# Linear attention and an expert FFN on one core: output weights' operands kept in DRAM, some products' results in one-bank tiles

## The chip, the cores and the metric

The kernel runs on one core of one Trainium2 chip. The metric is the device time of one execution in microseconds; of the kernel before, three runs are given by their median. Within the core, PE is TensorE (matmuls; PEld is its loading of weights), DVE is VectorE, ACT is ScalarE, POOL is GpSimd and SP is SyncE, which here only issues DMAs.

## The reference

4096 tokens of 1024 features are normalised (`xn`). A linear attention and a mixture-of-experts FFN are computed from `xn`, and the output is `x + attention * silu(ffn)`:

```
q, k, v  = xn @ Wq.T + bq, xn @ Wk.T + bk, xn @ Wv.T + bv
phi(t)   = elu(t) + 1
context  = phi(q) * cumsum(phi(k) * v, over tokens) / 8
s        = context @ Wo.T + bo
g        = silu(p * (gelu(xn @ w1.T + b1) @ w2.T + b2))   # tokens that a top-2 router with a capacity keeps
out      = x + s * g
```

All experts share one FFN. A token that no expert keeps has g = 0, so its output is x. The kernel computes attention output and FFN only for a list of 2048 chosen tokens, which the router fills in order of tokens.

## The kernel before, in words

**First part (to 445 us).** For the head of the tokens it normalises, transposes, routes, and computes keys and values with their running sums (`kvs` in DRAM). This part is not changed.

**Second part: 140 products.** The 2048 chosen tokens are handled in two passes of 1024 (`NP` = 2, loop at L1371). A pass is a row of ten big matrix products of 1024 x 1024 x 1024: for each of four quarters of the FFN, `hidden` (1024 hidden units by 1024 tokens) and `ffn_out`; then `queries` and `result`. Each is computed by a scheme with seven half-size products in place of eight (512 x 512 x 512), whose operands are sums of quarters of the two matrices. So a pass has 70 products and the kernel 140. In pass 0, the quarter s has `hidden` at products 14s+1 to 14s+7 and `ffn_out` at 14s+8 to 14s+14; `queries` are products 57 to 63 and `result` 64 to 70.

**One product.** `multiply(n)` (L1010) issues 48 matmuls of 128 x 128 by 128 x 512. An fp32 operand is kept as two fp32r parts: a rounded one, which ACT casts (`Unit.cast`, L799), and the rest, which DVE subtracts (`Unit.low`, L802). Three matmuls (high by high, high by low, low by high) make one fp32 product. An operand comes in two halves u of 8 KB a partition, in three rotating slots per side, so the first half of product n+1 can be made when n begins, and the second when n is done with its first half. Left operands (`a`) are weights in `hidden` and `queries`, tokens' features in `ffn_out` and `result`. Right operands (`b`) are tokens in the former, weights in the latter. The right tokens' seven sums are split once and kept in DRAM (`xtd`); `fetched` (L986) loads them by SP's queue. Those of pass 1 are made in pass 0 by `xprep_items` (L656): four items, each gathering rows, transposing, summing, splitting, and storing seven operands' pieces through POOL's queue. They use the pool `s4` of eight 4 KB buffers (`small`).

**Results.** Several products add into one PSUM tile, a chain. `chains` (L1039) groups them; two tiles of four banks (`fps`) take turns. After product n, DVE or ACT reads its tile in the phase `evac` of n+1.

**The order of the work is written by hand.** For each n, the loop at L1390 issues the matmuls of product n and then runs the hooks of ten phases in order: load, pre, cast0, evac, low0, add, cast1, low1, post, raw. Within a phase they run in the order in which `on` registered them. PE, DVE, ACT and SP keep this order; so does POOL for what is marked `in_turn`. `cast0`, `low0`, `cast1`, `low1` at n make the operands of n+1. The hooks of `xprep_items` are registered at the top of a pass, ahead of all others of that pass.

**Around queries and result.** `queries` calls `features` with `act` (Relu and Exp on ACT, L1248) and `then` (L1260: the rest of elu + 1, then times the running sums, six DVE instructions). `result` (L1300) calls `outputs`, which calls `left_tokens` (L1098: sums of the context's quarters), `right_weights` (L1072: four loads of `wo`, four sums on DVE, and casts and lows of both halves of seven operands; here with `ahead` = 1, so that its first two sums stand in the phase post of product 61) and `chains`. `done` (L1322) adds a finished quarter to `out` by four indirect DMAs of POOL; `last` (L1355) finishes a quarter.

Of the kernel before, what the change touches and what calls it, by code (L numbers as in the profile page):

```python
# [18 lines left out]
P = 128  # L19
# [8 lines left out]
BT = 512  # L28
# [18 lines left out]
def tile_first_tokens(  # L47
# [42 lines left out]


    xtd = [dp.tile([7 * P, 2 * 4 * BT], F32, name=f"xtd_{p}") for p in range(NP)]


    ident = kp.tile([P, P], F32, name="ident")
# [560 lines left out]
    def xprep_items(p, buf):  # L656
# [50 lines left out]

        return [item(j) for j in range(NJ)]


    def kv_srcs(blocks):
        return [w[e] for _ in range(blocks) for e in range(DC) for w in (wk, wv)]
# [66 lines left out]
    def name(n):  # L779
        uid[0] += 1  # L780
        return f"{n}_{uid[0]}"
# [127 lines left out]
        (f"{side}2", fp.tile([P, 2, 2 * BT], F32R, tag=f"{side}2", name=f"{side}2"))  # L909
        for side in "ab"  # L910
    )
    fps = ctx.enter_context(tc.tile_pool(name="fps", bufs=2, space=PSUM, reuse_waits="tile"))
    bq1, nbq = (cp.tile([P, DC], F32, name=n) for n in ("bq1", "nbq"))
    nc.gpsimd.tensor_scalar(bq1, bq, 1.0, None, ALU.add)
    nc.gpsimd.tensor_scalar(nbq, bq, -1.0, None, ALU.mult)
# [4 lines left out]
    def on(n, phase, f):  # L920
        hooks.setdefault((n, phase), []).append(f)
# [61 lines left out]
            on(n - 1, f"cast{u}", cast)  # L983
            on(n - 1, f"low{u}", lambda u=u: units[u].low())

    def fetched(n, p, i):  # L986

        units = plan_at(n)["b"]

        def load():  # L990
            src = tokens(p, i)
            for u in range(2):
                x = units[u] = Unit("b", 2 * n + u)
                nc.sync.dma_start(flat(x), src[u])

        on(n - 1, "load", load)
        plan_at(n)["bview"] = all_chunks

    def tokens(p, i):
        return xtd[p].rearrange("(i p) (u f) -> i u p f", i=7, u=2)[i - 1]  # L1000

    def flat(x):
        return x.t.bitcast(F32).rearrange("p h f -> p (h f)")
# [1 line left out]
    def plan_at(n):  # L1005
        while len(plan) < n:
            plan.append({"a": {}, "b": {}})
        return plan[n - 1]

    def multiply(n):  # L1010
        s = plan_at(n)
        if s["first"]:
            s["ps"][0] = fps.tile([P, 4, BT], F32, tag="ps", bufs=2, name=name("ps"))
        ps = s["ps"][0]
        order_of = [(u, m) for u in range(2) for m in range(4)]
        if n == len(plan):

            order_of.sort(key=lambda um: um[1])
        for u, m in order_of:
            a, b = s["aview"](s["a"][u].t), s["bview"](s["b"][u].t)  # L1020
            for k in range(2):
                for i, (h, l) in enumerate(((0, 0), (0, 1), (1, 0))):
                    nc.tensor.matmul(  # L1023
                        ps[:, m],
                        a(h, k, m),
                        b(l, k),
                        start=s["first"] and u == 0 and k == 0 and i == 0,
                        stop=u == 1 and k == 1 and i == 2,
                        skip_group_check=True,
                    )  # L1030
# [5 lines left out]
    FIRST = (1, 2, 6, 7, 5, 4, 3)  # L1036
    COLS = (1, 2, 6, 5, 7, 3, 4)

    def chains(n0, order, groups):  # L1039
        where = {i: [None] for g in groups for i in g[:1]}  # L1040
        for g in groups:
            for i in g:
                k = order.index(i)
                plan_at(n0 + 1 + k).update(first=i == g[0], ps=where[g[0]])

    def left_weights(n0, src, order):

# [21 lines left out]
        for k, i in enumerate(order):  # L1069
            built(n0 + 1 + k, "a", lambda i=i: q[of[i]], by_blocks, of_blocks)  # L1070

    def right_weights(n0, src, ahead=0):  # L1072

        q = dict(zip(((0, 0), (0, 1), (1, 1), "t", (1, 0)), raw))
        raw[:] = (q[k] for k in ("t", (0, 1), (0, 0), (1, 1), (1, 0)))

        def load(*keys):
            for i, j in keys:
                nc.sync.dma_start(
                    q[i, j].rearrange("p (a k) f -> p a (k f)", a=2),  # L1080
                    src[j, 2 * i : 2 * i + 2].rearrange("a p k f -> p a (k f)"),
                )

        on(n0 - 4, "raw", lambda: load((0, 0), (0, 1)))
        on(n0 - 3, "raw", lambda: load((1, 1)))
        on(n0 - 1, "raw", lambda: load((1, 0)))

        def t1():
            sub(q["t"], q[0, 1], q[0, 0])
            sub(q[0, 1], q[1, 1], q[0, 1])  # L1090

        on(n0 - 1 - ahead, "post" if ahead else "add", t1)
        on(n0, "post", lambda: sub(q[0, 0], q[1, 1], q["t"]))
        on(n0 + 5, "add", lambda: sub(q[1, 0], q[1, 0], q[0, 0]))
        for k, key in enumerate(((0, 0), (1, 0), (0, 0), "t", (0, 1), (1, 1), (1, 0))):
            built(n0 + 1 + k, "b", lambda key=key: q[key], by_chunks, all_chunks)

    def left_tokens(n0, h):  # L1098


        on(n0 + 1, "post", lambda: plus(h["t"], h[0, 1], h[1, 1]))
        on(n0 + 2, "pre", lambda: sub(h[0, 1], h[0, 0], h[0, 1]))
        on(n0 + 2, "pre", lambda: sub(h[0, 0], h["t"], h[0, 0]))
        on(n0 + 4, "add", lambda: sub(h[1, 0], h[1, 0], h[0, 0]))
        for k, key in enumerate(((0, 0), (1, 0), (0, 0), "t", (0, 1), (1, 0), (1, 1))):
            built(n0 + 1 + k, "a", lambda key=key: h[key], by_chunks, of_chunks)

    def right_tokens(n0, p, order):
        if n0:
            for k, i in enumerate(order):  # L1110
                fetched(n0 + 1 + k, p, i)
            return

        x = {(i, j): work[:, 2 * j + i] for i in range(2) for j in range(2)}
        t2 = hq["t"]
        on(3, "add", lambda: sub(x[0, 0], x[1, 1], t2))
        on(4, "add", lambda: sub(x[1, 0], x[1, 0], t2))
        keys = {1: (0, 0), 2: (1, 0), 3: (1, 1), 4: (1, 0), 5: (0, 0), 7: (0, 1)}
        for k, i in enumerate(order):
            built(1 + k, "b", lambda i=i: t2 if i == 6 else x[keys[i]], by_chunks, all_chunks)  # L1120

            def keep(k=k, i=i):
                for u in range(2):
                    nc.sync.dma_start(tokens(p, i)[u], flat(plan_at(1 + k)["b"][u]))

            on(k + 1, "raw", keep)

    def features(n0, p, src, act, then=None, order=ROWS):
# [2 lines left out]
        left_weights(n0, src, order)  # L1131
        right_tokens(n0, p, order)
        if order == ROWS:
            chains(n0, order, ((1, 2), (6, 7, 4), (5, 3)))
        else:
            chains(n0, order, ((1,), (2,), (6, 5, 3), (7, 4)))
        ps = {k: plan_at(n0 + k)["ps"] for k in range(1, 8)}
# [2 lines left out]
            nc.scalar.copy(whole(h[key]), whole(ps[1][0]))  # L1140

        def more(k, key, base):
            plus(h[key], ps[k][0], h[base])

        def c11():
            act(h[0, 0], ps[3][0], 0, 0)
# [22 lines left out]
            on(n0 + 5, "evac", lambda: more(4, (1, 1), (0, 1)))  # L1169
        on(n0 + 6, "evac", lambda: last(5, (1, 1), (1, 1)))  # L1170
        on(n0 + 7, "evac", lambda: last(6, (1, 0), (1, 0)))
        on(n0 + 8, "evac", lambda: last(7, (0, 1), (0, 1)))
        return h

    def over_blocks(row):
# [9 lines left out]
            n0, p, w1[s * DC : (s + 1) * DC], act, order=ROWS if s else FIRST  # L1185
        )

    def outputs(n0, h, src, ahead=0):
        left_tokens(n0, h)
        right_weights(n0, src, ahead)  # L1190
        chains(n0, COLS, ((1,), (2,), (6, 7, 4), (5, 3)))
        return {k: plan_at(n0 + k)["ps"] for k in range(1, 8)}

    def ffn_out(n0, h, s, y):


        ps = outputs(n0, h, w2[s])
        new = list(yq) if s == 0 else []

        def first(k, key, j):  # L1200
# [25 lines left out]
    def queries(n0, p):  # L1226
# [18 lines left out]
                    )  # L1245


        def act(dst, src, i, j):  # L1248
            if dst is src:
                r = [small("ex") for _ in range(2)]  # L1250
                r = [r[m // 2][:, m % 2 * BT : (m % 2 + 1) * BT] for m in range(4)]
            else:
                r = [dst[:, m] for m in range(4)]
            kvt["r", i, j] = r
            for m in range(4):
                e = 4 * i + m
                nc.scalar.activation(r[m], src[:, m], AF.Relu, bias=nbq[:, e : e + 1], scale=-1.0)
                nc.scalar.activation(r[m], r[m], AF.Exp, scale=-1.0)
# [40 lines left out]

    def result(n0, h, y, p):  # L1300

        ps = outputs(n0, h, wo[0], 1)
        c = {}

        def row():
# [13 lines left out]
            c[0] = y[0]  # L1319
            plus(c[0], ps[1][0], over_blocks(c["b"][:, :BT]))  # L1320

        def done(key, parts):  # L1322
            i, j = key
            for m in range(4):
                src = parts(m)
                apart(
                    in_turn(
# [20 lines left out]

        def more(k, key):
            c[key] = h["t" if key == (0, 1) else (0, 1)]  # L1350
            for half in range(2):
                v = slice(2 * half, 2 * half + 2)
                plus(c[key][:, v], ps[k][0][:, v], c[1][half])

        def last(k, key, base):  # L1355
            rows_of = range(4) if n0 + k == len(plan) else [slice(0, 4)]
            for v in rows_of:
                plus(c[base][:, v], ps[k][0][:, v], c[base][:, v])
                nc.vector.tensor_tensor(c[base][:, v], c[base][:, v], y[key][:, v], ALU.mult)
            done(key, lambda m: c[base][:, m])  # L1360

        on(n0 + 2, "evac", e1)
        on(n0 + 3, "evac", c11)
# [6 lines left out]
    n0 = 0  # L1370
    for p in range(NP):  # L1371
        y = dict(yq)
        if p + 1 < NP:
            prep = xprep_items(p + 1, small)
            ats = ((0, 2, 2, 2, 2, 3, 3, 3, 4), (2, 4, 4, 5, 4, 5, 5, 6, 6))
            for j, (s, at) in enumerate((s, at) for s in (1, 2) for at in ats):
                for k, (d, f) in enumerate(zip(at, prep[j])):
                    on(n0 + 14 * s + d, "post" if k else "load", f)
        for s in range(NQ):
            h = hidden(n0, p, s)  # L1380
            ffn_out(n0 + 7, h, s, y)
            n0 += 14
        h = queries(n0, p)
        finals(n0, y, p)
        result(n0 + 7, h, y, p)
        n0 += 14
# [87 lines left out]
```

## Time and profile before

| | |
|---|---|
| median of three runs | 2052.49 us (2051.97 to 2054.68) |
| profiled execution | 2053.1 us, its span 2051.3 us |
| PE busy | 1968.8 us, 96% of the span |
| DVE busy | 1513.0 us, 74% |
| ACT busy | 756.7 us, 37% |
| POOL busy | 398.3 us, 19% |
| matmuls of the products (L1023) | 6720, first at 444.7 us, last at 2029.6 us |
| granted clock, mean | 0.982 |
| DMA | 360.31 MB, 176 GB/s mean |

The span runs from the first to the last instruction of the execution. Busy time is that of an engine's instructions; a busy PE says that matmuls follow each other. A wait is put down to the instruction whose signal came last before the waiting one began. The granted clock is the share of full speed that TensorE was given.

### The profile page before, as it was taken

How to read it: one execution, taken by the hardware profiler on the slowest of the kernel's cores; microseconds unless marked ns; L12 is line 12 of the kernel's file. 1: busy time of each engine (PE TensorE's matmuls, PEld its weight loads, DVE VectorE, ACT ScalarE, POOL GpSimd, SP SyncE). 2: the span in 40 equal slices, each digit the busy share in tenths (PEclk: the TensorE clock that was granted, in tenths of full speed). 3: DMA queues.
4: the chain of work that ended last, by engine and by line, in shares of the span. 5: the costliest groups of instructions: out<-in, count | busy, mean ns of one | idle time of the engine just before them, and what ended most of it. 6: DMA issues, size and time to landing. Idle time of an engine off the chain costs nothing.

```text
span 2051.3 us, 22262 instructions
## 1 busy us (share of the span) xinstructions
PE 1968.8 (96%) x8840; PEld 1624.9 (79%) x8840; DVE 1513.0 (74%) x1378; ACT 756.7 (37%) x874; POOL 398.3 (19%) x359
## 2 busy tenths in 40 slices
PE   7999999999999999999999799999999999999875
PEld 6877878888887887888888578888888888888664
DVE  7868876679867867875877786775774775786784
ACT  2323332225433524433433453342432432433451
POOL 1001104654002402713040027300000003040013
PEclk9999999999999999999999989999999999999988
DMA  8867848657249349347156049427326327336314
GB/s 308 241 195 239 268 124 189 194 153 299 80 166 362 108 164 343 121 153 282 46 184 254 23 110 307 168 75 249 127 87 249 116 100 257 116 124 235 124 21 63
DMA packets 113842, 360.31 MB, mean 176 GB/s; under 512 B 12768, under 2 KB 37344, under 8 KB 95584
## 3 DMA queue, kind: packets, MB, share of 16 engines
q1 hardware_dynamic: 77504, 299.98, 42.2%
q0 software_dynamic: 17792, 42.55, 7.8%
q10 hardware_dynamic: 18432, 16.26, 3.5%
q8 instruction: 72, 1.18, 0.2%
q14 instruction: 42, 0.34, 0.1%
HBM read 292.66 MB, written 73.42 MB: 178 GB/s over the span
## 4 chain that ended last, share of the span: by engine, by line
PE 78%; DVE 11%; ACT 3%; DMA 3%; issue 3%; POOL 0%; ACTq 0%; SPq 0%; DVEq 0%; POOLq 0%
PE ps L1023 62%; PE pk L160 3%; PE pk L161 3%; PE pk L162 3%; PE pv L162 2%; PE pv L160 2%; PE pv L161 2%; DMA b<-xtd 1%; DVE hid L951 1%; DVE a L802 1%; DVE hid L1263 1%; DVE b L802 1%; DVE raw L948 1%; DMA xtd<-b 1%; PE pl L326 1%
## 5 line engine op out<-in xcount | busy, mean ns | idle before, releaser
L1023 PE MATMUL ps<-b,a 128*128 128x512 f32 x6720 | 1541.1, 392 | 44.2 <-DVE y L951 20.7
L1023 PEld LDWEIGHTS ps<-b,a 128*128 128x128 f32 x6720 | 1269.0, 189 | 315.9 <-ACT b L799 21.5
L799 ACT CAST a<-raw 128x1024 fp32r<-128x1024 f32 x140 | 147.2, 1052 | 434.6 <-PE ps L1023 376.1
L802 DVE TENSOR_TENSOR a<-raw,a 128x1024 fp32r<-128x1024 f32 x140 | 170.6, 1221 | 171.2 <-ACT a L799 171.2
L648 POOL DMA_INDIRECT gk<-kvs,eighth x128 | 156.4, 1222 | 657.8 <-DVE kv L240 620.0
L799 ACT CAST a<-hid 128x1024 fp32r<-128x1024 f32 x120 | 126.0, 1050 | 358.0 <-PE ps L1023 250.4
L802 DVE TENSOR_TENSOR a<-hid,a 128x1024 fp32r<-128x1024 f32 x120 | 146.5, 1221 | 63.8 <-ACT a L799 63.6
L802 DVE TENSOR_TENSOR b<-raw,b 128x1024 fp32r<-128x1024 f32 x140 | 170.7, 1220 | 1.9 <-ACT b L799 1.9
L951 DVE TENSOR_TENSOR hid<-ps,hid 128x2048 f32<-128x2048 f32 x54 | 123.5, 2286 | 54.4 <-PE ps L1023 54.4
L948 DVE TENSOR_TENSOR raw<-raw,raw 128x2048 f32<-128x2048 f32 x70 | 160.3, 2289 | 1.0
L799 ACT CAST b<-raw 128x1024 fp32r<-128x1024 f32 x140 | 146.6, 1047 | 2.1 <-DMA xtd<-b 2.1
L951 DVE TENSOR_TENSOR work<-ps,work 128x2048 f32<-128x2048 f32 x40 | 91.5, 2288 | 48.8 <-PE ps L1023 48.8
L160 PE MATMUL pk<-xt,ws_w 128*128 128x512 f32 (+1 forms) x264 | 102.4, 388 | 1.5 <-ACT xt L166 1.5
L161 PE MATMUL pk<-xt,ws_w 128*128 128x512 f32 (+1 forms) x264 | 102.0, 386 | 1.3 <-DVE xt L167 1.3
L162 PE MATMUL pv<-xt,ws_w 128*128 128x512 f32 (+1 forms) x264 | 101.4, 384 | 1.3 <-DVE ws_w L167 1.2
L162 PE MATMUL pk<-xt,ws_w 128*128 128x512 f32 (+1 forms) x264 | 101.8, 386 | 0.0
L160 PE MATMUL pv<-xt,ws_w 128*128 128x512 f32 (+1 forms) x264 | 101.6, 385 | 0.0
L161 PE MATMUL pv<-xt,ws_w 128*128 128x512 f32 (+1 forms) x264 | 101.2, 383 | 0.0
L166 ACT CAST ws_w<-wr_w 128x1024 fp32r<-128x1024 f32 x64 | 66.1, 1049 | 70.0 <-issue 30.8
L167 DVE TENSOR_TENSOR ws_w<-wr_w,ws_w 128x1024 fp32r<-128x1024 f32 x64 | 77.8, 1215 | 14.7 <-ACT ws_w L166 14.7
L680 POOL DMA_DIRECT2D xtd<-o x28 | 24.2, 888 | 283.3 <-DVE o L167 276.3
L362 ACT ACTIVATE kb<-pk,bs 128x512 f32<-128x512 f32 (+1 forms) x40 | 25.8, 645 | 140.8 <-PE pk L162 106.5
(185 smaller groups left out, 1656.4 us busy)
## 6 DMA issues: line engine op xcount, KB each, us to landing
b<-xtd SPq DMA_DIRECT2D x126, 1024.0 KB, 5.5
raw<-in_w SPq DMA_DIRECT2D x64, 1024.0 KB, 5.2
wr_w<-in_wk SPq DMA_DIRECT2D x32, 512.0 KB, 4.6
wr_w<-in_wv SPq DMA_DIRECT2D x32, 512.0 KB, 4.6
xtd<-b SPq DMA_DIRECT2D x14, 1024.0 KB, 7.7
xtd<-o POOLq DMA_DIRECT2D x28, 512.0 KB, 9.1
kvs<-kr ACTq DMA_DIRECT2D x32, 256.0 KB, 4.9
raw<-in_wq SPq DMA_DIRECT2D x8, 1024.0 KB, 5.1
```

Source lines behind the costliest of these rows:

```text
L160: nc.tensor.matmul(ps, ws[:, 0, k], mv[:, 0, k, c0:c1], start=k == 0, stop=False)
L161: nc.tensor.matmul(ps, ws[:, 0, k], mv[:, 1, k, c0:c1], start=False, stop=False)
L162: nc.tensor.matmul(ps, ws[:, 1, k], mv[:, 0, k, c0:c1], start=False, stop=k == DC - 1)
L166: nc.scalar.copy(dst[0], src)
L167: nc.vector.tensor_tensor(dst[1], src, dst[0].bitcast(F32), ALU.subtract)
L362: nc.scalar.activation(kb, ps, AF.Identity, bias=bcol)
L648: nc.gpsimd.indirect_dma_start(out=dst, out_offset=None, in_=src, in_offset=bass.IndirectOffsetOnAxis(ap=idx, axis=0),)
L799: nc.scalar.copy(self.parts[0], src)
L802: nc.vector.tensor_tensor(self.parts[1], self.src, self.parts[0].bitcast(F32), ALU.subtract)
L948: nc.vector.tensor_tensor(dst, a, b, ALU.subtract)
L951: nc.vector.tensor_tensor(dst, a, b, ALU.add)
L1023: nc.tensor.matmul(ps[:, m], a(h, k, m), b(l, k), start=s["first"] and u == 0 and k == 0 and i == 0, stop=u == 1 and k == 1 and i == 2, sk ...
```

## The change

It has these parts.

- **Weights' right operands in DRAM.** `wod`, in DRAM, holds the seven right operands of `wo` in split form. `wprep_items` makes them during pass 0, in four items. An item fetches 4 x 256 KB, forms sums of 128 x 512 (four subtractions), splits seven pieces, and stores each (512 KB) through POOL. The stages stand at products k (fetch, phase load) and k+1, k+1, k+2, k+3, k+4 (phase post) for k = 8, 20, 25, 37, and are registered at the top of pass 0. `result` then takes `right_stored`, which fetches the operands from `wod` with `fetched`, in both passes, in place of `right_weights`.
- **Stages for pass 1's tokens** begin at products 13 and 30 where they began at 14 and 28.
- **Places in PSUM.** A chain's tile is taken from one of two places (`banks`), the one that the preceding product does not write. Where `apart` is set, the tile is four tiles of one bank each: for the chain of products 61 and 63 in `queries` (5 and 3 in the scheme's numbers), and in the last result for the chain of its products 3, 5 and 7. The last product of such a chain computes one block after the other.
- **Reading by blocks.** In `queries`, the last product's quarter is read block by block, each followed by its Relu and Exp: blocks 0 to 2 within product 63 (phases add, low1, post), block 3 in phase pre of 64. In the last result, quarters 5, 6 and 7 of the order are finished and scattered block by block.
- **One subtraction moved.** In `left_tokens`, the sum for `h[0, 1]` is formed one product later, from other terms.

```diff
+    def wprep_items(w, buf):
+        def item(a, k):
+            v = {}
+            def fetch():
+                for j in range(2):
+                    r = buf(f"wr_{a}_{k}_{j}")
+                    for i in range(2):
+                        v[i, j] = r[:, i * BT : (i + 1) * BT]
+                        row = w[j, 2 * i + a].rearrange("p k f -> p (k f)")
+                        in_turn(nc.gpsimd.dma_start(v[i, j], row[:, k * BT : (k + 1) * BT]))
+            def out_of(i, src):
+                o = buf(f"wo_{a}_{k}_{i}")
+                oh = o.bitcast(F32R).rearrange("p (h t) -> h p t", h=2)
+                split((oh[0], oh[1]), src)
...
+                in_turn(
+                    nc.gpsimd.dma_start(dst[:, a, :, k], o.rearrange("p (h t) -> p h t", h=2))
+                )
+            def sums():
+                t = buf(f"wt_{a}_{k}")
+                v["t1"], v["t2"] = t[:, :BT], t[:, BT:]
+                nc.vector.tensor_tensor(v["t1"], v[0, 1], v[0, 0], ALU.subtract)
+                nc.vector.tensor_tensor(v["t2"], v[1, 1], v["t1"], ALU.subtract)
+            def out1():
+                out_of(1, v[0, 0])
+                out_of(2, v[1, 0])
+            def out2():
+                out_of(6, v["t2"])
+                nc.vector.tensor_tensor(v[1, 0], v[1, 0], v["t2"], ALU.subtract)
+                out_of(4, v[1, 0])
+            def out3():
+                out_of(3, v[1, 1])
+                nc.vector.tensor_tensor(v[0, 1], v[1, 1], v[0, 1], ALU.subtract)
+                out_of(7, v[0, 1])
+            def out4():
+                out_of(5, v["t1"])
+            return fetch, sums, out1, out2, out3, out4
+        return [item(a, k) for a in range(2) for k in range(2)]
...
+    def banks(apart):
+        i = last_place[0] = 1 - last_place[0]
+        place = places[i]
+        if place[0] != apart:
+            place[2].close()
+            place[:2] = apart, place[2].enter_context(
+                tc.tile_pool(
+                    name=name("fps"), bufs=1, space=PSUM, side=("left", "right")[i],
+                    reuse_waits="tile",
+                )
+            )
...
     def multiply(n):
         s = plan_at(n)
         if s["first"]:
-            s["ps"][0] = fps.tile([P, 4, BT], F32, tag="ps", bufs=2, name=name("ps"))
+            s["place"][0], s["ps"][0] = banks(s["apart"])
+        last_place[0] = s["place"][0]
...
-        if n == len(plan):
+        if s["apart"] and s["last"]:
...
+    def right_stored(n0, ops):
+        for k, i in enumerate(COLS):
+            fetched(n0 + 1 + k, ops, i)
...
-        on(n0 + 2, "pre", lambda: sub(h[0, 1], h[0, 0], h[0, 1]))
         on(n0 + 2, "pre", lambda: sub(h[0, 0], h["t"], h[0, 0]))
+        on(n0 + 3, "pre", lambda: sub(h[0, 1], h[1, 1], h[0, 0]))
...
-        on(n0 + 8, "evac", lambda: last(7, (0, 1), (0, 1)))
+        if not then:
+            on(n0 + 8, "evac", lambda: last(7, (0, 1), (0, 1)))
+            return h
+        def block(m):
+            key = (0, 1)
+            plus(h[key][:, m], ps[7][0][m], h[key][:, m])
+            act(h[key], h[key], *key, blocks=(m,))
+        for d, phase, m in ((7, "add", 0), (7, "low1", 1), (7, "post", 2), (8, "pre", 3)):
+            on(n0 + d, phase, lambda m=m: block(m))
...
-        ps = outputs(n0, h, wo[0], 1)
+        ps = outputs(n0, h, right_stored, wod, final=p == NP - 1)
...
-            done(key, lambda m: c[base][:, m])
+                done(key, lambda m: c[base][:, m], range(4) if len(parts) == 1 else (v,))
...
+        if p == 0:
+            for k, f in zip((8, 20, 25, 37), wprep_items(wo[0], small)):
+                for d, stage in zip((0, 1, 1, 2, 3, 4), f):
+                    on(n0 + k + d, "post" if d else "load", stage)
...
-            for j, (s, at) in enumerate((s, at) for s in (1, 2) for at in ats):
+            for j, (k, at) in enumerate((k, at) for k in (13, 30) for at in ats):
```

## The prediction

> **What bounds the kernel now.** I read the waits of TensorE first, because PE is busy for 96% of the span and ends the chain of waits. Columns: total us, times, longest.
>
> ```profile
> PE ps L1023 <- DVE y L951: 20.7, 2, 10.5
> PE ps L1023 <- DVE b L802: 8.4, 8, 1.4
> PE ps L1023 <- DVE hid L951: 8.1, 2, 4.0
> PE ps L1023 <- DMA b<-xtd: 5.6, 3, 2.5
> ```
>
> All that the 140 products wait for is here, 44 us, in few places. I then cut the span at the starts of products (every 48th matmul) and read windows. Columns: stretch, length, busy PE, PEld, DVE, ACT, POOL, granted clock, DMA share, GB/s.
>
> ```profile
> 630.20:643.40 13.20, 11.12 (x50) 8.90 (x49) 8.04 (x9) 6.19 (x10) 3.40 (x4) 1.00 1.01 394
> 643.40:656.00 12.60, 12.60 (x49) 10.23 (x50) 8.65 (x10) 4.71 (x7) 2.53 (x3) 0.86 1.02 408
> ...
> 1140.40:1157.50 17.10, 11.60 (x49) 8.67 (x47) 13.11 (x13) 8.07 (x12) 0.00 (x0) 0.96 0.01 1
> 1157.50:1182.60 25.10, 13.18 (x49) 10.13 (x49) 21.02 (x17) 11.40 (x15) 0.00 (x0) 0.77 0.00 0
> 1182.60:1198.10 15.50, 14.09 (x49) 11.02 (x50) 13.65 (x12) 12.82 (x19) 7.22 (x4) 0.76 0.37 50
> 1198.10:1209.00 10.90, 10.90 (x50) 9.03 (x49) 9.19 (x7) 5.55 (x7) 0.00 (x0) 1.00 0.49 126
> ```
>
> An undisturbed product takes 10.88 us (last row). I number products 1 to 140; per pass of 70, queries are 57-63 and result 64-70. Products 64, 65, 66 take 17.2, 25.1 and 15.5; with 1.1 before 62 that is 26.3 us over the 10.88s, and the same stretch of pass 1 loses 26.5. VectorE is full there. Products 18 and 32 wait for DMA and the next ones lose 1.7 each to a half-speed clock: 4.0 and 4.4 us. Product 10 waits 0.7. The timeline shows who is late at the transition:
>
> ```profile
> 1137.07 2.28 DVE L951 TENSOR_TENSOR hid<-ps,hid 128x2048 f32<-128x2048 f32 x1
> ...
> 1155.10 2.28 DVE L951 TENSOR_TENSOR hid<-ps,hid 128x2048 f32<-128x2048 f32 x1
> ...
> 1157.53 0.76 PE L1023 MATMUL ps<-b,a 128*128 128x512 f32 x1 [4.03 <-DVE hid L951]
> ```
>
> Product 63 ended at 1140.7; its result is read only at 1155.10, as VectorE does the query features, a subtraction of output weights and their splits first. Product 65 needs that place. The tail:
>
> ```profile
> 2029.98 0.69 DVE L951 TENSOR_TENSOR y<-ps,y 128x512 f32<-128x512 f32 x1 [6.26 <-PE ps L1023]
> ...
> 2038.19 1.56 POOL L1328 DMA_INDIRECT out<-y,half  x1 [0.30 <-issue]
> ```
>
> The first quarter of the last product is read only when all of it is done (PE ends at 2029.8), though its blocks were computed one after another.
>
> **Part 1: output weights from DRAM.** Per result stage it removes 4 subtractions (2.29) and 14 splits on DVE (1.22), 26.2 us, 14 casts on ACT (1.05), and four 1 MB loads. Once, in pass 0, it adds 28 casts (0.62), 28 lows and 16 subtractions (0.69): ACT 17, DVE 30 us, 16 loads and 28 stores on POOL's queue. DVE falls by 22 us, but only its place counts.
>
> The stored operands come by SP's queue, 2 MB per product. Nearest row: the 1 MB b<-xtd, 5.5 us to landing against 10.9 per product, so hidden; with the next quarter's 1 MB that is 289 GB/s, where 394 was moved above. If that cover were gone, the saturated row below (11.9 us) says some 2.5 per product. Product 62's 1.1 us goes: the wo load at L1079 no longer stands in SP's queue ahead of its b.
>
> **Part 2: the transition, with one-bank tiles and the moved subtraction.** Durations from the timeline: read 2.29, four Relu/Exp pairs 5.1, `then` 5.05, low 1.13, cast 1.05, block read 0.69, block pair 1.3. DVE is free at 1117.8, not 1122.4 (the two weight subtractions, 4.62, are gone).
> - 61 read until 1120.1, ACT pairs 1125.3, cast and low 1127.5, `then` 1132.6.
> - 62 read until 1134.9, left split 1136.0: 64 starts as 63 ends, 1139.2. Blocks 0 and 1 are read by 1137.3, inside product 63. ACT, in order: pairs 1140.1, block 0 1141.5, cast 1142.5, block 1 1143.8. Low 1143.7, `then` 1148.8, blocks 2 and 3 by 1150.2.
> - ACT: last pairs 1152.3, cast of 65's left operand 1153.3, low 1154.5: 65 starts at 1154.5, 4.4 us after 64 ends. Behind the wait for its pairs, DVE has nothing else to do in time.
> - `then` 1160.6, sum 1162.9, one subtraction (two before) 1165.2, both reads of 64 (4.6) 1169.8, low 1171.0: 66 starts at 1171.0 (before: 1182.6 and, after a split, 1184.8).
>
> Clock: the Trainium skill ("TensorE: Matmul & The Clock Gate", Part 1) says that half speed comes after at least one idle window of about 3.4 us. The 643.40 row speaks otherwise: after 2.2 us idle the clock was 0.86 over the product, 1.7 us lost. By the rule 65 (4.4 idle) pays some 2.4 and 66 (3.2 idle) nothing; by the row 66 pays 1.7 too. I take the row: 67 starts at 1171.0 + 10.9 + 1.7 = 1183.6, against 1198.1. Gain 14.5; pass 1, which lost 0.3 more, 14.8. Sum -29.3 (-20 if ACT's order costs a few us more, -36 if no half-speed stretch is left).
>
> A right slot of 64 comes free late, as block order keeps both halves of 63's operands until 7/8 of it: its b lands at 1144.2 for 1144.6. A miss of up to 4 us costs nothing, since 65 waits for DVE anyway.
>
> **Part 3: the tail.** Product 139's blocks are read and scattered one by one from 9.3 us before PE's end T. Eight scatters at 1.87: first issue T-8.6, last T+4.5, still POOL-bound; before, the last issue was T+8.4. -3.9 (0 to -6).
>
> **Part 4: pass 0 pays.** The new stages are registered ahead of the products' own, so they precede them within a phase.
> - Output stages: from product 10 on, DVE has 9.0 of 10.9 us, plus 2.7 per new stage with its wait for ACT. Worked like the above, product 11 is 0.4 late, 24 and 25 0.9 and 0.8: +2.1; product 10's 0.7 goes with the moved subtraction. Bounds -0.7 to +8.
> - The second pair of token items moves from products 28-34 to 30-36. Its DMA no longer meets the 2 MB weight load in 31:
>
> ```profile
> DMA packets 1681, 7.81 MB, mean 391 GB/s; under 512 B 149, under 2 KB 149, under 8 KB 1306
> ...
> b<-xtd SPq DMA_DIRECT2D x4, 1024.0 KB, 11.9
> ```
>
>  That is the DMA view of 625-645: saturated. Products 31 to 34 now ask 4.0, 4.5, 3.5, 4.5 MB = 16.5 MB in 43.5 us (before, 10 MB fell in two products). The skill ("DMA: Bandwidth & Descriptors", Specifications) puts HBM at about 358 GB/s per core: 46.1 us, 2.6 late, which speaks against the move; the row's 394 gives 41.9. I take the row: product 33's 4.4 us goes. The first pair moves by one product only: 17 and 18 still ask 5.5 and 4.5 MB, so 19 stays late, 4.0.
> - But its last stages now fall in products 34-36, where DVE already has 9 us each. In 34: 9.0 + 6.0 (two transposes 1.25, three lows and two sums 0.69) and 1 of waiting for ACT; in 35: 9.0 + 2.8 + 1.9. With 1.4 brought along from 33, the read of product 35 starts 9.0 us into 36 (before, 0.8: 835.17). From there to the split for product 38 it was 19.8 us; minus 2.3 (moved subtraction), plus 2.6 (token stage of 36 ahead of the sum): 20.1. Ready at 29.1, due at 21.8: 7.3 late over products 37 and 38, and some 1.9 of half clock. +9.2 (0 if DMA makes the token stages slip into free time, 14 if 36's lag spreads).
>
> **Edits at nothing.** The choice of place: the waits show none for a place at an output-to-hidden border, so there was no such stall to remove; the same tile was waited for at 65, and is after. The moved subtraction costs nothing in its new phase in passes without new stages: products 24 and 38 have 2.8 and 3.1 us of DVE idle before.
>
> **Sum.** -29.3 - 3.9 + 2.1 - 0.7 - 4.4 + 9.2 = -27.0. The profiled execution took 2053.1 (span 2051.3), 0.6 over the median of 2052.5; off the median: 2025.5.
>
> **Rivals.**
> - *Pass 0 doesn't pay* (0.22): DVE slips the token stages into its 5 us of idle time in 30 and 32. Then +9.2 and +2.1 fall away: 2014. For: 32 and 33 had 5.5 and 3.4 us idle. Against: in order, stages can't go earlier than their phase.
> - *ACT takes DVE's place at the transition* (0.18): pairs, casts and block pairs share one queue; if each link costs 1 to 2 us more, and half-speed stretches stay, the gain is 15-20 for both: 2035 to 2040. For: DVE waited 5.10 for ACT there at 1130.88.
> - *Slower* (0.05): the pool of eight 4 KB buffers. ACT's casts for stored tiles wait in order for a buffer whose POOL store has not landed:
>
> ```profile
> ACT o L166 <- DMA xtd<-o: 18.9, 4, 7.0
> ```
>
>  If each of the 16 new stages stopped ACT 7 us, some 3 us beyond the products' slack, that is 48: 2068. It decides from 2.2 us per stage (34 us). Against: output stages move 0 to 99 GB/s, the row is from saturated stretches.
> - *No effect* (0.03): the transition waits for a link I took as gone; the gain stays under 4 us.
> - My case (0.52): own range 2019 to 2032.
>
> **How the numbers follow.** Differences under 0.2% (4 us) can't be told from none here. 2025.5 is the likeliest; the range 2011 to 2039 takes in the first two rivals' most. Faster 0.92, same 0.03, slower 0.05.
>
> **What would show it.** Right: no wait for y at L951 of 10 us; product 65 starts some 3 to 5 us late and 66 again, at half clock; the b<-xtd waits fall from 3 to 1; the last scatter is issued 4 to 5 us after PE's end; PE waits for a split at products 37 and 38. Wrong: waits for ACT at the casts of o or for b<-wod, PE idle in products 9-13 or 22-29 by more than 5 us, or a transition gain outside 10 to 18 per pass.

## The result, and the profile after

The kernel after takes 2029.72 us (median of four runs, 2027.63 to 2031.69), the kernel before on the same chip 2053.59: ratio 0.9884, interval 0.9867 to 0.9901. That is 23.9 us less; 27.0 was forecast, and 2025.5. The profiled execution took 2027.63, with a span of 2025.7 for 2051.3: 25.6 us less.

That gain is the one of this chip. On the two chips of most experiments below, runs scattered by some 10 us and took longer: the kernel before 2073 to 2074 on both, the kernel after, which ran on one of them, 2070 (ratio 0.9974, 0.9956 to 0.9993). There the change gains 4 us and not 24. The runs `made_and_stored` and `after_again` show what was different; single stages are compared where no such disturbance lies.

This is what each stage of products lost over 10.88 us per product, from the starts of the products (every 48th matmul), with the start of product 1 and the time from PE's end to the span's end:

```
            start   1-13  14-20  21-30  31-34  35-45  46-60  61-70  71-130  131-139  140   PE's end to span's end
before      444.7    0.6    4.0    0.0    4.4    0.0    0.0   26.3     0.0     26.5   0.0   21.5
after       449.3    0.1    4.8    1.6    0.0    6.6    0.1   11.1     0.1      9.0   2.4   17.4
```

The waits of TensorE for its products after (total us, times, longest; shorter ones left out). The wait for `hid` of 8.1 us is gone, that for `b<-xtd` fell from 5.6 to 3.6. The wait for `y`, 20.7 us before, is the first line here, with 9.2:

```profile
PE ps L1104 <- issue: 9.2, 2, 4.6
PE ps L1104 <- DVE b L855: 4.4, 4, 1.7
PE ps L1104 <- DMA b<-xtd: 3.6, 2, 2.9
...
PE ps L1104 <- DVE kb L403: 2.7, 1, 2.7
PE ps L1104 <- ACT a L852: 2.2, 2, 1.1
PE ps L1104 <- SPq L1520: 2.1, 1, 2.1
```

The two waits put down to "issue" are those of products 66 and 136. The timeline below shows for what: 66 starts 0.1 us after the end of DVE's second read of product 64's result (into `y`), which sets that product's place in PSUM free. It is the wait for `y` of the kernel before, at less than half its length. Windows of single products (columns as before): 37, 64, 65, 66.

```profile
847.70:862.90 15.20, 13.01 (x49) 10.02 (x49) 13.18 (x11) 7.67 (x11) 3.88 (x6) 0.89 0.39 107
...
1148.00:1160.10 12.10, 11.02 (x50) 8.81 (x48) 7.53 (x10) 6.35 (x10) 0.00 (x0) 1.00 0.71 258
1160.10:1176.70 16.60, 11.46 (x49) 8.88 (x49) 16.50 (x14) 5.34 (x6) 0.00 (x0) 0.95 0.54 185
1176.70:1190.30 13.60, 13.60 (x49) 10.63 (x50) 11.29 (x9) 10.06 (x17) 5.63 (x4) 0.81 0.33 88
```

DVE is full in 65 alone (16.50 of 16.60); before, it was busy for 34.1 of the 42.2 us of 64 and 65. PE is idle for 5.1 us in 65 and then runs at a clock of 0.81 through 66. The timeline of the transition:

```profile
1126.47 2.48 DVE L1031 TENSOR_TENSOR hid<-ps,hid 128x512 f32<-128x512 f32 x4
...
1143.01 1.28 DVE L1031 TENSOR_TENSOR hid<-ps,hid 128x512 f32<-128x512 f32 x2
...
1155.66 1.28 DVE L1031 TENSOR_TENSOR hid<-ps,hid 128x512 f32<-128x512 f32 x2
...
1160.03 0.73 PE L1104 MATMUL ps<-b,a 128*128 128x512 f32 x2 [1.08 <-ACT a L852]
...
1174.25 2.28 DVE L1031 TENSOR_TENSOR y<-ps,bo 128x2048 f32<-128x2048 f32 x1
...
1176.63 13.72 PE L1104 MATMUL ps<-b,a 128*128 128x512 f32 x48 [4.62 <-issue]
```

The last quarter of the queries is read in 2 + 2 blocks, the first two while product 63 runs (it ends at 1148.0); before, all four were read at 1155.10, 14.4 us after 63 had ended. Product 65 waits 1.1 us, 66 waits 4.6. The tail:

```profile
1998.59 9.78 PE L1104 MATMUL ps<-b,a 128*128 128x512 f32 x42 [2.14 <-SPq L1520]
2000.44 0.68 DVE L1031 TENSOR_TENSOR y<-ps,y 128x512 f32<-128x512 f32 x1
...
2010.71 1.56 POOL L1431 DMA_INDIRECT out<-y,half  x1 [0.30 <-issue]
```

The first block of product 140 is read 8 us before PE's end (2008.4). But PE stands for 2.1 us in the middle of its first block: block by block, it needs the second half of the fetched right operand after 6 matmuls, not after 24. That load was issued at 1989.67 and landed 8.8 us later, at 1998.45, so the wait is for it, though the profile puts it down to SyncE (L1520). The last scatter is issued 2.3 us after PE's end, for 8.4 before.

### The profile page after: what moved, and what is told of

Its sections match the earlier page's. It is cut to its first block, busy times and chain, and to the rows that moved or that the text cites. A ratio compares the mean times of both kernels' runs of the same rounds, so it can differ in the third digit from the quotient of the medians.

```text
span 2025.7 us, 22443 instructions
## 1 busy us (share of the span) xinstructions
PE 1965.6 (97%) x8840; PEld 1623.2 (80%) x8840; DVE 1491.0 (74%) x1412; ACT 745.6 (37%) x874; POOL 414.9 (20%) x403
## 5 line engine op out<-in xcount | busy, mean ns | idle before, releaser
L1104 PE MATMUL ps<-b,a 128*128 128x512 f32 x6720 | 1535.5, 391 | 26.3 <-issue 9.2
L650 POOL DMA_INDIRECT gk<-kvs,eighth x128 | 152.2, 1189 | 587.3 <-DVE kv L242 549.2
L1031 DVE TENSOR_TENSOR hid<-ps,hid 128x2048 f32<-128x2048 f32 (+1 forms) x69 | 124.8, 1821 | 59.6 <-PE ps L1104 59.6
L1028 DVE TENSOR_TENSOR raw<-raw,raw 128x2048 f32<-128x2048 f32 x62 | 141.8, 2288 | 0.8
L855 DVE TENSOR_TENSOR b<-raw,b 128x1024 fp32r<-128x1024 f32 x112 | 136.4, 1218 | 1.6 <-ACT b L852 1.6
L852 ACT CAST b<-raw 128x1024 fp32r<-128x1024 f32 x112 | 117.3, 1047 | 1.8 <-DMA xtd<-b 1.8
L1031 DVE TENSOR_TENSOR work<-ps,work 128x2048 f32<-128x2048 f32 x40 | 91.4, 2285 | 31.2 <-PE ps L1104 31.2
L1283 ACT ACTIVATE hid<-hid,bs 128x512 f32<-128x512 f32 x104 | 66.7, 713 | 24.6 <-DVE hid L1031 24.6
```

The source lines that it names most:

```text
L650: nc.gpsimd.indirect_dma_start(out=dst, out_offset=None, in_=src, in_offset=bass.IndirectOffsetOnAxis(ap=idx, axis=0),)
L852: nc.scalar.copy(self.parts[0], src)
L855: nc.vector.tensor_tensor(self.parts[1], self.src, self.parts[0].bitcast(F32), ALU.subtract)
L1028: nc.vector.tensor_tensor(dst, a, b, ALU.subtract)
L1031: nc.vector.tensor_tensor(dst, a, b, ALU.add)
L1104: nc.tensor.matmul(ps[m] if s["apart"] else ps[:, m], a(h, k, m), b(l, k), start=s["first"] and u == 0 and k == 0 and i == 0, stop=u == 1 ...
```

## The experiments

Eight of the twelve ran on one chip (the kernel before there: 2073.2 and 2073.4 us; the kernel after did not run there); `after_again`, `first_left_again` and `spread2` ran on another (before: 2074.1), and `before_again` on one where before takes 2052.4. Three hold the transition's two parts apart and the price in pass 0.

### made_only: the operands made again, the blocks kept

```diff
-        ps = outputs(n0, h, right_stored, wod, final=p == NP - 1)
+        ps = outputs(n0, h, lambda n, s: right_weights(n, s, 1), wo[0], final=p == NP - 1)
-        if p == 0:
+        if False:
```

`right_weights` has its parameter `ahead` again, as before; the last two lines of the diff take away the items of `wprep_items`.

> The changed kernel, but the result's right operands are made from wo in both passes as before, and nothing of wo is stored; one-bank tiles, moved subtraction and stage times stay. My theory (VectorE's removed work at the transition carries the gain): the two sums (4.6), the later sum (2.3) and some five splits on the chain (5.7) come back, so product 66 starts 12 to 13 us later in each pass; the stores' 1.6 in pass 0 go. About 2053, close to the kernel before. Rival (reading by blocks carries the gain): about 2036.

2072.79 us, ratio to before 0.9992 (0.9971 to 1.0013). In the stages: products 61 to 70 lose 21.3 us and 131 to 139 21.5, for 11.1 and 9.0 after. Products 64 and 65:

```profile
1163.52:1182.45 18.93, 11.62 (x49) 8.75 (x47) 12.47 (x14) 11.48 (x17) 0.00 (x0) 0.97 0.00 1
1182.45:1200.43 17.98, 13.63 (x48) 10.43 (x49) 17.88 (x16) 6.35 (x7) 0.00 (x0) 0.85 0.00 0
```

ACT is busy for 11.48 us of product 64 and DVE for all of 65, and the waits name who is late:

```profile
PE ps L1104 <- ACT b L852: 13.4, 4, 6.2
PE ps L1104 <- DVE b L855: 11.6, 9, 1.7
```

These are the right operand's casts and splits, which stand in both queues among those of the queries. So of the 15 to 17.5 us that a pass gains here, 10 to 12.5 come with the making of the weights. Product 62 starts 1.2 us late again, with the load of `wo` again ahead of its operand in SP's queue.

### made_and_stored: the same, but the operands are also stored and not fetched

The diff is that of `made_only` without its last two lines.

> As made_only, but the seven operands of wo are also made and stored in pass 0 as in the changed kernel, and never fetched. The difference to made_only is the price of making them. My theory: 2 to 4 us, in products 24, 25, 37 and 38 (about 2056). Rival (waits for the eight small buffers): over 10 us, with waits of ScalarE for wod.

2089.50 us, ratio 1.0084 (1.0055 to 1.0114). Beside `made_only` this shows the price of the 28 stored pieces alone: 16.7 us on this chip, where 2 to 4 were expected. In the undisturbed stages it is 1.6 us: products 24 and 25, 0.9 and 0.7, as in the kernel after. In the profiles the rest lies in products 46 and 47 (18.7 us, where `made_only` loses 0.2; 71 to 130, also disturbed, lose 5.0 for 15.5). They hold no stage of the new items, but they hold work that these pushed there. POOL gathers rows of the running sums (`gk`) as soon as its queue gets to them. In the kernel before that is at once after the last store of the token items:

```profile
824.48 1.72 POOL L680 DMA_DIRECT2D xtd<-o  x2 [9.86 <-DVE o L167]
826.50 1.01 POOL L648 DMA_INDIRECT gk<-kvs,eighth  x1 [0.30 <-issue]
...
930.98 0.94 POOL L648 DMA_INDIRECT gk<-kvs,eighth  x1 [50.04 <-DVE kv L240]
```

In the kernel after, the stores of the fourth item of `wo` stand ahead of the gathers and wait for DVE:

```profile
909.40 0.71 POOL L733 DMA_DIRECT2D wod<-wo  x1 [6.61 <-DVE wo L169]
910.42 1.01 POOL L650 DMA_INDIRECT gk<-kvs,eighth  x1 [0.31 <-issue]
```

So 32 gathers that ran in products 35 to 40 (37 to 42 in `made_only`) run in 42 to 45, and with the 16 that follow they make one row of 48 up to product 48; in `made_and_stored` likewise. On the first chip the long row costs PE nothing (46 to 60 lose 0.1). On the two others all profiles with it but one lose 6.9 to 23.6 us there (`spread` 1.4), and `made_only`, without it, 0.2. That the new stages bring the loss about is shown by the times of this pair of runs; that it comes by the pushed gathers is what the profiles suggest, and how gathers would slow PE is not shown.

### whole_read: the operands fetched, the last quarter of the queries read whole

```diff
-            chains(n0, order, ((1, 2), (6, 7, 4), (5, 3)), then is not None)
+            chains(n0, order, ((1, 2), (6, 7, 4), (5, 3)))
-        if not then:
+        if True:
```

> The changed kernel with the queries' last chain in one four-bank tile, computed half by half and read whole as before; operands from DRAM stay. By the prediction's steps, product 65 then starts 1 to 3 us earlier (its cast stands ahead of the four Relu/Exp pairs), but the last pairs end later and 66 starts 1 to 3 us later: about 2033. Rival (the blocks carry the transition): 10 us per pass, about 2050.

2077.03 us, ratio 1.0007 (0.9984 to 1.0031). The transitions lose 13.7 and 12.0, for 11.1 and 9.0: the blocks are worth 2.6 to 3.0 us per pass. Products 64 and 65:

```profile
1183.22:1194.10 10.88, 10.88 (x50) 9.01 (x49) 9.08 (x9) 3.36 (x5) 0.00 (x0) 1.00 0.57 193
1194.10:1215.20 21.10, 11.65 (x50) 8.62 (x48) 15.90 (x14) 9.90 (x14) 0.00 (x0) 0.91 0.44 149
```

Product 64 loses nothing and 65 10.2, where after they lose 1.2 and 5.7. PE's time in 65 is 11.65 of 21.10: it waits 0.5 us within 65 and 8.9 before 66 (after: 1.1, 0.5 and 4.6). As expected, 65 starts earlier with the read left whole, and 66 later.

### sub_back: the moved subtraction put back

```diff
+        on(n0 + 2, "pre", lambda: sub(h[0, 1], h[0, 0], h[0, 1]))
         on(n0 + 2, "pre", lambda: sub(h[0, 0], h["t"], h[0, 0]))
-        on(n0 + 3, "pre", lambda: sub(h[0, 1], h[1, 1], h[0, 0]))
```

> The changed kernel with the subtraction for h[0, 1] back in front of the one for h[0, 0]. Theory: 2.3 us more on the chain to product 66 in each pass and to products 24 and 38, and some 1 at product 10, with some more half-speed clock: about +10, 2040. Rival (other links hide it): under 3.

2078.31 us, ratio 1.0018 (1.0003 to 1.0034). One DVE instruction of 2.3 us, one product earlier in ten output stages, costs only where DVE has no slack: 1.7 and 3.4 us at the transitions (12.8 for 11.1, 12.4 for 9.0), 4.4 in products 21 to 30 (24 alone loses 4.8 for 0.9) and 4.4 in 35 to 45. That is 13.9 us against the first profile of the kernel after, 10.7 against `after_again` (both ran on other chips). In the other output stages it costs nothing.

### items_14_28: the token items at their former products

```diff
-            for j, (k, at) in enumerate((k, at) for k in (13, 30) for at in ats):
+            for j, (k, at) in enumerate((k, at) for k in (14, 28) for at in ats):
```

> The changed kernel with the stages for pass 1's tokens at products 14 and 28, as before. Theory: DMA is late again at product 33 (4.4), the 6.6 us at products 37 and 38 fall to under 2: about -1, 2028.5. Rival (37 and 38 are late because of wo's stages, not the moved ones): they stay, and 33 is added: 2034.

2060.14 us, ratio 0.9949 (0.9927 to 0.9970). The products 32, 33 and 37:

```profile
800.25:816.51 16.26, 11.05 (x50) 8.86 (x48) 9.04 (x11) 6.72 (x11) 3.42 (x4) 0.94 1.01 401
816.51:829.89 13.38, 13.38 (x49) 10.86 (x50) 8.47 (x10) 4.27 (x6) 2.57 (x4) 0.81 0.91 346
862.53:873.41 10.88, 10.88 (x50) 9.01 (x49) 10.85 (x8) 4.01 (x4) 0.00 (x0) 1.00 0.01 2
```

Product 32 is late for its operand with DMA at 401 GB/s (5.4 us), 33 pays 2.5 at half clock, and 37 runs undisturbed. In the kernel after it is the other way round. The move swaps a DMA wait (7.9 us here, 4.4 in the kernel before) for a DVE wait (6.6). It isn't shown to pay: products 14 to 45 lose 13.6 us here, and 16.1 to 17.8 in `made_and_stored`, `whole_read`, `first_left` and `last_by_halves`, which have the stages of the kernel after on the same chip.

### first_left and first_left_again: the products' first tile in the other place

```diff
-    last_place = [0]
+    last_place = [1]
```

> The changed kernel with the first product in the other of the two places. In the changed kernel product 1 waits 2.7 us for VectorE's read of the keys' and values' last tile (kb), which the kernel before didn't. Theory: the right place lies on the banks of that tile, so this wait goes and nothing else moves: -2.9, about 2026.8. Rival: the wait is that product 1 follows closely on the first part's end in any place: no change.

> The changed kernel with the first product in the left place, beside the changed kernel itself. Theory: product 1 loses its wait for kb (2.7) and the half-speed clock after it (1.7): about 0.002 less. Rival: no change.

2066.42 us on one chip, ratio 0.9952 (0.9931 to 0.9974); 2066.93 on the other, 0.9954 (0.9932 to 0.9977). PE's wait of 2.7 us for `kb` is gone from both profiles. The kernel before doesn't have it; in the kernel after it is:

```profile
448.68 0.44 DVE L403 SCALAR_TENSOR_TENSOR kb<-pv,bs,kb 128x256 f32<-128x256 f32 x1
...
449.27 2.97 PE L1104 MATMUL ps<-b,a 128*128 128x512 f32 x12 [2.69 <-DVE kb L403]
```

DVE's last read of the tile `pv` of the first part precedes product 1's first matmul: with `last_place` 0 the first chain gets the place over that tile, with 1 it doesn't. On the chip where both ran, the time of `first_left_again` can't be told from that of `after_again` (0.9954 and 0.9974, intervals overlapping); the wait is shown, its gain in the median isn't.

### last_by_halves: product 140 not block by block

```diff
-        if s["apart"] and s["last"]:
+        if s["apart"] and s["last"] and n < len(plan):
```

> The changed kernel with product 140 computed half by half, its four one-bank tiles still read and scattered one by one. In the changed kernel PE waits 2.1 us within product 140 for the second half of its fetched operand. Theory: that wait goes, but POOL's queue of eight scatters sets the end, so the span falls by 0.4 only. Rival (PE's end sets the tail): -2.4.

2066.30 us, ratio 0.9970 (0.9952 to 0.9988). Product 140 loses 0 for 2.4, but from PE's end to the end of the span it is 20.3 us for 17.4. PE ends at 2037.7 here, and POOL has issued scatters without a pause of more than 0.3 us since 2028.73; the last scatter is issued 5 us after DVE's read of its block:

```profile
2037.92 0.69 DVE L1031 TENSOR_TENSOR y<-ps,y 128x512 f32<-128x512 f32 x1
...
2042.94 1.56 POOL L1431 DMA_INDIRECT out<-y,half  x1 [0.30 <-issue]
```

From the start of product 140 to the end of the span it is 31.2 us here, 30.7 after, 32.4 before. So POOL's eight scatters set the end, and to take PE's wait out of 140 gains nothing.

### spread and spread2: the new stages put where DVE has room

```diff
-    last_place = [0]
+    last_place = [1]
-        if s["apart"] and s["last"]:
+        if s["apart"] and s["last"] and n < len(plan):
-            for k, f in zip((8, 20, 25, 37), wprep_items(wo[0], small)):
+            for k, f in zip((8, 22, 25, 36), wprep_items(wo[0], small)):
-            ats = ((0, 2, 2, 2, 2, 3, 3, 3, 4), (2, 4, 4, 5, 4, 5, 5, 6, 6))
-            for j, (k, at) in enumerate((k, at) for k in (13, 30) for at in ats):
+            at = (0, 2, 2, 2, 2, 3, 3, 3, 4)
+            for j, k in enumerate((13, 16, 27, 30)):        # spread2: (13, 16, 30, 41)
```

> The changed kernel with the first product in the left place, product 140 by halves, wo's items at products 8, 22, 25, 36, and the four token items each over five products, at 13, 16, 27, 30. Theory: the waits at product 1 (2.9), 19 (4.8 with its half-speed clock), 24 and 25 (1.6), 37 and 38 (6.6) go: about -16, 2014. If DVE has no room for the token items in products 18 to 20 and 32 to 34, 22 or 36 and later are late: 2020.

> The changed kernel with the left place first, product 140 by halves, wo's items at products 8, 22, 25, 36, and token items of five products each at 13, 16, 30, 41, so that no two meet the weight loads of the third quarter. Theory: the waits at products 1 (2.7 and clock 1.7), 24 and 25 (1.6), 33 (none, where spread had 7.7), 37 and 38 (6.6) are gone, 19 stays at 4: some 12 us under the changed kernel, 0.982 of the kernel before. If the running sums' gathers from product 42 leave the item at 41 too few buffers, products 44 to 46 are late instead.

`spread`: 2049.80 us (six runs, 2035.73 to 2060.59), ratio 0.9905 (0.9876 to 0.9934). `spread2`: 2062.10, ratio 0.9923 (0.9899 to 0.9948); on its chip the kernel after has 0.9974 (0.9956 to 0.9993), so it is faster, by 7.9 us of the 12 expected. The profile of `spread` is that of its fastest execution. In both, products 24, 25, 37, 38 and 140 lose nothing, and PE doesn't wait for `kb`. `spread` still loses 7.7 in 32 and 33, where DMA is saturated as in `items_14_28`. `spread2` loses nothing there, and 22.9 in product 45. Its timeline shows why:

```profile
950.94 0.62 ACT L168 CAST o<-x 128x512 fp32r<-128x512 f32 x1 [12.90 <-DMA xtd<-o]
...
964.75 0.94 POOL L650 DMA_INDIRECT gk<-kvs,eighth  x1 [0.31 <-issue]
965.69 1.86 POOL L682 DMA_DIRECT2D xtd<-o  x2
969.86 0.62 ACT L168 CAST o<-x 128x512 fp32r<-128x512 f32 x1 [15.05 <-DMA xtd<-o]
...
976.01 9.32 PE L1104 MATMUL ps<-b,a 128*128 128x512 f32 x27 [22.79 <-issue]
```

Its fourth item stores its pieces through POOL's queue, and gathers of rows stand there in the same products, most of them 1.25 us apart (16 from 944.41 to 964.75). Pieces that DVE had split at 951.59 and 954.85 are stored at 965.69 only. ACT, in order, waits for a buffer (12.90, then 15.05 us), and PE for what ACT and DVE do behind that. This is the forecast's slower rival, at a place where its condition holds; the expectation had named it. A fourth item in another place was not tried.

### after_again and before_again: the two kernels a second time

> The changed kernel itself, beside the other two, as their measure: 0.988 of the kernel before, waits at products 1, 19, 24, 25, 37, 38, 140 as in its first profile.

> The kernel before, unchanged, profiled a second time. On the two chips of the experiments it took 2073 to 2074 us, where its first three runs took 2052.5, and the unchanged kernel after took 2070 there where it first took 2029.7. First theory: single matmuls of products 45 to 48 and 74 to 76 lose time there to gaps of 1.1 to 2 us for which the profile shows no signal that PE waits for, in the changed kernel and in its variants; on such a chip the kernel before loses some 20 us in the same way, less than the 22 us of the changed kernel's products, so that 2053 + 20 = 2073. Then the stretches 46 to 60 and 71 to 130 of this run lose 10 to 20 us over 10.88 per product, where they lost 0.0 in the first profile. Rival: the products of the kernel before are undisturbed on any chip (0 to 1 us in these stretches), only the changed kernel's transfers meet the gaps, and the 20 us lie in the first part, so that product 1 starts at 460 to 465 us where it started at 444.7. If the chip is one on which the kernel before takes 2053 again, neither is told apart, and the stretches lose 0.

`after_again`: 2069.98 us, ratio 0.9974 (0.9956 to 0.9993), on a chip where before takes 2074.1. `before_again` took 2051.67 on a chip where before takes 2052.4, with stages as in the first profile (61 to 70 lose 26.3, 131 to 139 26.6, the others 3.0 in 14 to 20 and 4.4 in 31 to 34). So it didn't meet a disturbance, and whether before loses its 20 us in the same way is not shown.

The transitions of `after_again` lose 11.1 and 10.1 (after: 11.1 and 9.0). What it loses beside that lies in the first part (product 1 starts at 459.3 for 449.3), in 31 to 34 (3.7 us for 0), 35 to 45 (8.6 for 6.6), 46 to 60 (7.7) and 71 to 130 (14.4). Product 75 of `after_again`, and then of the kernel after in its first profile:

```profile
1303.33:1328.18 24.85, 16.64 (x49) 11.08 (x50) 4.56 (x3) 2.00 (x2) 10.44 (x12) 0.73 0.51 184
```

```profile
1278.76:1289.63 10.87, 10.87 (x49) 9.01 (x48) 4.65 (x3) 2.11 (x2) 8.43 (x9) 1.00 0.97 355
```

Product 46 of `first_left` took 31.75 us, at a clock of 0.72. In all of these POOL issues gathers of rows (`gk`) one after the other. On the first chip that costs PE nothing. On the others PE makes gaps of 0.2 to 2.2 us between single matmuls, put down to nothing that the profile shows, and the clock falls. The row of gathers at 72 to 76 is the same in both kernels; the long one at 42 to 48 only the kernel after has (`made_and_stored`). That speaks for the gathers as the reason that the gain shrinks from 24 to 4 us there, but no run shows the kernel before on such a chip stage by stage.

## Why the prediction was right, point by point

The account of the 25.6 us: transitions -15.2 and -17.5, the tail -1.7 (-4.1 after PE's end, +2.4 in product 140), 31 to 34 -4.4, 1 to 13 -0.5; against that the start of product 1 +4.6, 14 to 20 +0.8, 21 to 30 +1.6, 35 to 45 +6.6, 46 to 130 +0.2. Sum -25.5.

- **Transition: -14.5 and -14.8 forecast, -15.2 and -17.5 measured.** The order of the steps held: DVE works through the queries' features, then 64's reads, and 66 comes late at half clock. The sizes of the steps were not: 65 starts 1.2 us late and not 4.4. ACT's first Relu came at 1127.30, 0.8 after the read of product 61 began, since that chain also lies in one-bank tiles and is read in four blocks; I had let ACT wait for the whole read. That took some 2 us off everything behind. Another 1.2 us is that 65 begins as soon as its cast is done, with the two matmuls that need no split, where I had let it wait for the split. 66 waits 4.6 us, not 3.2, for both reads of 64, as forecast, and loses 2.7 (pass 0) or 2.0 more, mostly at half clock, for 1.7.
- **The clock: the rule fails, and the row is no rule either.** The wait before 66, 4.6 us, is beyond the 3.4 us of the Trainium skill ("TensorE: Matmul & The Clock Gate", Part 1), so both would slow it. Shorter waits went both ways. In the kernel after product 18 waits 2.9 us, and 19 takes 12.60 us at a clock of 0.86, as in the row; but product 140 waits 2.1 us and keeps its clock at 1.00. And the second profile of the kernel before has the wait of the row again (13.10 less 11.07, 2.0 us), without the slow product behind it:

```profile
630.00:643.10 13.10, 11.07 (x49) 8.82 (x47) 7.93 (x9) 6.18 (x10) 3.41 (x4) 1.00 1.01 390
643.10:654.60 11.50, 11.13 (x48) 8.93 (x48) 8.35 (x9) 3.74 (x6) 2.13 (x3) 1.00 1.02 409
```


  So a wait of some 2 us can cost half speed or not, and what decides isn't shown. That 19 paid 1.7 again, as forecast, was partly luck.
- **The weights.** Removing their making was the larger part: `made_only` gives back 10 to 12.5 us of a pass, `whole_read` 2.6 to 3.0. With the 1.7 and 3.4 us of the moved subtraction (`sub_back`) that makes 14.5 and 18.9, for a whole gain of 15.2 and 17.5; the three aren't independent, since all unload DVE in the same stretch.
- **The cover of the fetched operands: nearly.** Products 67 and 68 lose 0.6 (PE waits 0.4 for b<-wod) and 70 loses 0.8 (for b<-xtd, a wait that occurs twice and not once): 1.4 us in pass 0, none in pass 1, for nothing forecast.
- **Tail: -3.9 forecast, -4.1 after PE's end, but -1.7 from the start of product 140.** The last scatter comes 4.7 us after the end that PE would have had without its wait (forecast: 4.5). I had not asked when the second half of a fetched right operand is needed once the product runs block by block. `last_by_halves` shows that the wait has almost no price, as POOL is behind.
- **Pass 0's output stages: +2.1 forecast, +1.6 measured.** Product 11 lost nothing (0.4 forecast), 24 and 25 0.9 and 0.7 (0.9 and 0.8). The 0.7 of product 10 went, but not by the moved subtraction: `before_again` hasn't it, and `sub_back` doesn't bring it back.
- **31 to 34: -4.4 right on this chip.** DMA moved 380 to 408 GB/s in 32 and 33, and the operand came in time. The estimate from the 358 GB/s per core of the Trainium skill ("DMA: Bandwidth & Descriptors", Specifications) made it 2.6 late; the row's 394 decided rightly. Product 19 stayed late, 4.8 for 4.0. On the two other chips 31 to 34 lose 0 to 3.9 us in the runs with these stages, so some of the wait comes back there.
- **37 and 38: +9.2 forecast, +6.6 measured.** The mechanism was right: the read of product 35 began 8.6 us into product 36 (forecast 9.0), and the split of 38's right operand was done 28.4 us after 36's start (forecast 29.1, due at 21.8): 6.6 late for 7.3. The 1.9 of half clock didn't add to it: 37 runs at 0.89, but 38 waits for DVE anyway. `items_14_28` removes it, `sub_back` makes it 10.9. With -4.4 in 31 to 34 the move of the token items is a loss of 2.2 us, for 4.8 forecast.
- **"Edits at nothing": wrong in one of two.** The place of a chain costs 2.7 us in product 1. I looked at the borders between the products only, not at the border to the first part, whose last PSUM tile lies in one of the two places. The other 1.9 us of product 1's later start lie in the first part, which is the same program; most of it between 311 and 326 us, where the clock was 0.77, for 0.89 before. The moved subtraction was right: it costs nothing in its new place, and in its old one 11 to 14 us. A third was not named: the new stores' place in POOL's queue, ahead of the gathers. It costs nothing on the first chip; on another the new stages cost 16.7 us, most of it where the pushed gathers run (`made_and_stored`).
- **Rivals.** Pass 0 pays (8.5 of the forecast 10.6 us, by 1.6 + 6.6 + 0.8 less 0.5). ACT didn't take DVE's place: PE waits for its casts 2.2 us in all. The pool of buffers never stopped ACT for the new stages: the slower rival was wrong for this change and right for `spread2`.

The sum came within 1.4 us of the spans' difference because errors cancelled, which is luck: product 1 +4.6, the tail with product 140 +2.2 and 14 to 20 +0.8, against -3.4 at the transitions, -2.6 at 37 and 38 and some -0.4 in pass 0's output stages. In the medians, 23.9 against 27.0, the miss is 3.1. It was luck, too, that the first chip is one where the long row of gathers costs nothing: on the chip of `after_again` the gain is 4.1 us.

What stays open: why PE makes gaps beside POOL's gathers on two chips and not on the first. Both kernels have 128 of these gathers, the kernel after 48 of them in one row. Where the kernel before loses its 20 us on such a chip is not shown.

## What to carry to other kernels

What work costs in full queues is set by its place and not by its sum: 26 us of DVE and 15 of ACT per pass were 10 to 12 us on the path, and a subtraction of 2.3 us cost nothing in most stages and 4.4 in one stretch. Work that is moved to where the engines seem free must be followed through every queue that it enters: two token stages in products with 9.0 of 10.9 us of DVE taken cost 6.6, stores behind a row of gathers in POOL's queue cost 23, and where new stores pushed gathers back, the loss was 17 us on one chip and nothing on another. Where a sum of tiles is given a new place in PSUM, look at who had that place before, also beyond the part that is changed: here that was 2.7 us.

## What the runs showed of the hardware that was not expected

- Beside a long row of gathers on POOL, TensorE can lose time without any wait that the profile names, on some chips: product 75 took 24.85 us with a clock of 0.73 in `after_again`, and 10.87 at 1.00 on the first chip. What joins the two isn't shown.
- An idle stretch of TensorE of some 2 us was followed by half speed in one run of the kernel before (2.1 us, then a clock of 0.86) and by full speed in another (2.0 us, then 1.00).
- DMA moved 401 to 408 GB/s on one core over windows of 11 to 16 us.
- The two loads of 1 MB for product 140 took 6.0 and 8.8 us from issue to landing, with scatters in between. Block by block, the product needs the second one after 6 matmuls in place of 24, and it came 2.1 us too late.
